# A four-layer graph network on one core: layer 0 takes blocks 1 to 3 ahead of the heavy first block

## The chip, the core and the metric

The kernel runs on one core of a Trainium2 chip. The core has five engines with a queue of instructions each: TensorE (PE in the profile; its weight loads are listed apart as PEld), VectorE (DVE), ScalarE (ACT), GpSimd (POOL) and SyncE (SP, which here only starts transfers). [...] The metric is the device time of one execution in microseconds (us). Before the change it was 1721.15 us, the median of three runs (1717.11 to 1723.85). The profiled execution is longer, 1881.9 us from first to last instruction; times inside the program are read from that one, and the verdict is in the unprofiled times.

## What is computed

There are N = 3327 nodes with 512 features, and a 0/1 adjacency matrix with its entries set very unevenly: the chance of an edge between i and j falls with both indices as (1+i)^-0.5 (1+j)^-0.5, so the first rows have by far the most neighbours. Four layers follow each other, each as x = layernorm(x + layer(x, adj)):

```
layer 0  h = x W (8 heads of 64); e = leaky_relu(f1[i] + f2[j]) where adj[i,j] > 0
         softmax over the neighbours j, out = elu(sum of attention * h[j])
layer 1  relu([x W_self + b, mean of the neighbours W_nb + b] W_comb + b)
layer 2  leaky_relu(mean of the first 64 neighbours W_nb + b) + leaky_relu(x W_line + b)
layer 3  as layer 0, with 4 heads of 128 and quaternion weights
```

The change touches only layer 0 and what comes before it. In layer 0 every row's output is a softmax-weighted sum over that row's neighbours alone, so the blocks of rows can be taken in any order.

## The kernel before

**Tiling.** The 3327 rows are cut into NB = 26 blocks of 128 rows. For every block the kernel builds one or more *edge lists*: the (row, neighbour) pairs of the block, packed into *chunks* of 128 edges. Block 0, with most edges, has three lists of 14 chunks (`HEAVY`, 42 chunks); blocks 1, 2 and 3 have one list of 19, 15 and 13 chunks (47 together), and the later ones fewer, down to 5. The whole has 243 chunks.

**Building the lists** is the generator `structure`. For a block it fetches the adjacency rows in two halves (`fetch`, L839), turns them into 0/1 on ScalarE (`masks`, L846; block 0's go into a tile m0 that is kept, the others into two rotating tiles m), multiplies them with column codes on VectorE (L856), pulls the codes out eight at a time with max and match_replace on VectorE (L874, L876 in segments, L886, L888 over the candidates), and then spreads them over chunks with small matmuls (L902 to L925), ScalarE copies (L905 to L928) and VectorE operations (L932 to L939). Block 0 takes three rounds per segment and 120 slots per row and list, so its lists are long work for VectorE. The generator stops at a `yield` several times per block; the caller decides by `more(n)` how many such steps are placed between other work. By the code, block 0 has 31 steps, blocks 1 to 4 have 7 each, and all others 5.

**The prologue** (the first 220 us of the profile) places, for each block t of 26, one stage of a *projection* (load x, transpose on PE, 8 matmuls L995 in two passes, copies on ScalarE, store to the table t0_d in HBM) and three steps of `structure`. `fused_weights` (layer 1's weights multiplied together, L762) joins at t = 4, and `first_rows` at t = 10. `first_rows` turns m0 into the transposed masks row0 and near0 of block 0, which layers 1 to 3 use: a running count over m0 (L1323), a compare that limits it to the first 64 neighbours (L1326), and 52 transposes (L1332). `finish` then needs all projections and writes the table's two special rows (L1046); only after that may the first gather start.

**Layer 0's loop** goes over *groups* of up to four chunks of one block. A group (`Gat.group`) gathers its chunks' rows from t0_d with indirect transfers issued by GpSimd (L963, one per chunk, into a ring of 22 places `rows`), compares, makes scores with small matmuls (L1165, L1171), takes exponents on ScalarE (L1177, L1178), weighs the gathered rows on VectorE (L1185), and adds them up on PE with two matmuls per chunk in two passes each (L1193). After each group one or two steps of `structure` are placed. When a block's last chunk is in, `layer0_end` follows: normalisation on VectorE and ScalarE with a small piece on GpSimd (L777, L778), a transposition and 8 PE instructions by wn (L762) for layer 1's table t1_d, and for the first ten blocks 8 more by wx. Up to five groups and the ends of earlier blocks are in flight together.

**What sets the order.** Up to the end of layer 0 the program's text does not fix the order within an engine's queue: the framework's scheduler plans it from the dependencies, with the program's order as a preference. One sees it in the trace: the count L1323 is placed at t = 10, but runs at 27.8 us, between the steps of block 0's first list. After layer 0 (`tc.manual_schedule()`) the text's order holds.

**The ring's memory** is lent to the prologue first: m0 lies where places 0 to 3 of the ring are, then the weights, the scores' vectors, layer 1's raw weights, a zero row, and the running count so_far. Some 256 numbers at its end are not lent.

Of the kernel before, what the change touches and what calls it, by code (L numbers as in the profile page):

```python
# [9 lines left out]
BF16 = mybir.dt.bfloat16  # L10
# [8 lines left out]
ALU = mybir.AluOpType  # L19
# [4 lines left out]
P = 128  # L24
# [4 lines left out]
KEEP = 64.0  # L29
# [509 lines left out]
DENSE = 2  # L539
AHEAD = 2  # L540
LATE0 = 16
RING = 22 * 528
MORE = 3072
RANGE = 60.0
# [75 lines left out]
def sparse_path(ctx, tc, flag_i, x, adj, l0_w, l0_a1, l0_a2, l1_w_self, l1_b_self, l1_w_nb, l1_b_nb,  # L620
# [13 lines left out]
    nc = tc.nc  # L634
# [16 lines left out]
    dram = ctx.enter_context(tc.tile_pool(name="s_dram", bufs=1, space=DRAM))  # L651
    keep = pool_in(ctx, "s_keep")

    lists = []
    for b in range(NB):
        parts = HEAVY if b == 0 else ((0, SEGMENTS[b], CAPS[b], SLOTS[b], SEGMENTS[b], 1),)
# [168 lines left out]
    def structure(big, mid, ps, m0):  # L825
# [6 lines left out]
        def fetch(b):  # L832
            ab = abs_[b % len(abs_)]
            for s in range(2):
                w = min(HW, N - s * HW)
                if b == NB - 1:
                    nc.gpsimd.memset(ab[s][96:P, :], 0)
                for p0, p1 in rows_of(b):
                    nc.sync.dma_start(ab[s][p0:p1, :w], adj[b * P + p0:b * P + p1, s * HW:s * HW + w])  # L839
            return ab  # L840

        def masks(b, ab):
            ms = []
            for s in range(2):
                m = m0[:, s * HW:(s + 1) * HW] if b == 0 else big.tile([P, HW], BF16, name="m", bufs=2)
                nc.scalar.activation(m, ab[s], AF.Sign, accum_out=half[:, s, b:b + 1])  # L846
                ms.append(m)
            return ms

        ms = masks(0, fetch(0))  # L850
        yield None
        for b in range(NB):
            ab = fetch(b + 1) if b + 1 < NB else None
            val = big.tile([P, NP], U16, name="val")
            for s in range(2):
                nc.vector.tensor_mul(val[:, s * HW:(s + 1) * HW], ms[s], code[:, s * HW:(s + 1) * HW])  # L856
# [5 lines left out]
            for q, l in enumerate(lists[b]):  # L862
# [7 lines left out]
                for s in range(len(cuts) - 1):  # L870
                    seg = val[:, cuts[s]:cuts[s + 1]]
                    for r in range(rounds):
                        top = cand[:, s * rounds + r, :]
                        nc.vector.max(out=top, in_=seg)  # L874
                        if r + 1 < rounds:
                            nc.vector.match_replace(out=seg, in_to_replace=top, in_values=seg, imm_value=0.0)  # L876
                    if s == (len(cuts) - 1) // 2:
                        if q == 0 and ab is not None:
                            ms = masks(b + 1, ab)
                        yield None  # L880
                cf = cand.rearrange("p s e -> p (s e)")
                sl = mid.tile([P, K + 1], F32, name="sl")
# [34 lines left out]
                for c0 in range(0, L, G):  # L917
# [19 lines left out]
                    with nc.allow_low_precision(reason="whole numbers below 4096"):  # L937
                        nc.vector.tensor_reduce(l.idx[:, c0:c0 + g], eq, AX.X, ALU.add)
                    nc.vector.scalar_tensor_tensor(l.dst[:, c0:c0 + g], l.idx[:, c0:c0 + g], 0.0, v[:, :, 0],  # L939
                                                   ALU.is_gt, ALU.mult)  # L940
            yield b

    def groups(ring, blocks=range(NB)):

# [300 lines left out]
    def lent(n, dtype=F32):  # L1245

        nonlocal free
        at, free = free, free + n * mybir.dt.size(dtype) // 4
        return rows[:, at:free].bitcast(dtype)

    free = 0
# [5 lines left out]
    with ExitStack() as pro:  # L1257
        wp = pool_in(pro, "l0pw", side="right")
        xp = pool_in(pro, "l0px", 2, side="right")
        ps3 = pool_in(pro, "l0pp3", 3, space=PSUM)  # L1260
        ps2 = pool_in(pro, "l0pp2", 2, space=PSUM)
        ps1 = pool_in(pro, "l0pp1", 1, space=PSUM)

        ps = Banks(ps1, po=ps3, tr=ps2)
        banks = Banks(ps1, pv=ps2)
        m0 = lent(NP, BF16)
        made = structure(big, mid, banks, m0)
        w0 = lent(DC * (D + 3 * H0)).rearrange("p (c s o) -> p c s o", c=DC, s=2)
        for c in range(DC):
            for s in range(2):  # L1270
                nc.sync.dma_start(by_heads(w0, c, H0)[:, s],
                                  l0_w[s * H0 // 2:(s + 1) * H0 // 2, c * P:(c + 1) * P, :].rearrange("h p o -> p h o"))
        a0 = lent(2 * D).rearrange("p (s h o) -> p s h o", s=2, h=H0)
        for s, src in enumerate((l0_a1, l0_a2)):
            nc.sync.dma_start(a0[:, s].rearrange("p h o -> p (h o)"), row(src, H0 * OUT0))
        g0 = Gat("g0", t0_d, H0, OUT0, w0, 0)
        next(made)
        score_weights(w0, xp, a0, H0, OUT0)

        def projection(b):  # L1280
            load(xres[b], x, b)
            yield
            xt = transposed(xp, ps, xres[b], g0.xsum, b)
            yield
            pw = g0.products(ps, xt)
            yield
            g0.write(b, xp, pw)

        def fused_weights():

            wc = lent(2 * DC * D).rearrange("p (c o) -> p c o", o=D)
            nc.sync.dma_start(wc, l1_w_comb.rearrange("(c p) o -> p c o", p=P))
            bc = wp.tile([P, D], F32, name="bcomb")
            nc.sync.dma_start(bc, row(l1_b_comb, D))
            bs = wp.tile([P, 2 * DC, 1], F32, name="bs")
            with nc.allow_non_contiguous_dma(reason="two small biases"):
                nc.sync.dma_start(bs[:, :DC, 0], l1_b_self.rearrange("(c p) -> p c", p=P))
                nc.sync.dma_start(bs[:, DC:, 0], l1_b_nb.rearrange("(c p) -> p c", p=P))
            for s, (src, o) in enumerate(((l1_w_self, wx), (l1_w_nb, wn))):
                for i in range(DC):  # L1300
                    raw = xp.tile([P, D], F32, name="raw")
                    nc.sync.dma_start(raw, src[i * P:(i + 1) * P, :])
                    yield
                    rt = transposed(xp, ps, raw)
                    yield
                    po = times(ps, rt, wc[:, s * DC:(s + 1) * DC, :])
                    nc.scalar.copy(o[:, i, :], po)
            pb = ps.tile([P, D], F32, name="po")
            for k in range(2 * DC):
                bb = wp.tile([P, P], F32, name="bb", bufs=2)  # L1310
                nc.vector.tensor_copy(bb, bs[:, k].to_broadcast([P, P]))
                nc.tensor.matmul(pb, bb, wc[:, k, :], start=k == 0, stop=k == 2 * DC - 1)
            nc.vector.tensor_add(bias1, pb, bc)

        def first_rows():

            zero = lent(3 * D, BF16)[0:1, :]
            nc.gpsimd.memset(zero, 0.0)
            for r in range(2):
                nc.sync.dma_start(t1_d[r:r + 1, :], zero)  # L1320
                nc.sync.dma_start(t2_d[r:r + 1, :], zero)
            so_far = lent(NP, I16)
            nc.vector.tensor_tensor_scan(so_far, m0, m0, 0.0, ALU.add, ALU.bypass)  # L1323
            for o in (row0, near0):
                if o is near0:
                    nc.vector.scalar_tensor_tensor(m0, so_far, KEEP, m0, ALU.is_le, ALU.mult)  # L1326
                for c0 in range(0, NB, 8):
                    g = min(8, NB - c0)
                    yield
                    pt = banks.tile([P, 8, P], BF16, name="lp")  # L1330
                    for c in range(g):
                        nc.tensor.transpose(pt[:, c, :], m0[:, (c0 + c) * P:(c0 + c + 1) * P], ident16)  # L1332
                    nc.scalar.activation(o[:, c0:c0 + g, :], pt[:, :g, :], AF.Identity, saturate=False)

        ready, whole = -1, True

        def more(n=1):
            nonlocal ready, whole
            for k in range(n):
                b = next(made, None)  # L1340
                whole = b is not None or ready == NB - 1
                ready = ready if b is None else b

        fused = Stages()
        for t in range(NB):
            work.add(projection(t))
            work.step()
            more(3)
            if t == 4:
                fused.add(fused_weights())  # L1350
            if t == 10:
                fused.add(first_rows())
            fused.step()
        work.drain(more)
        fused.drain(more)
        g0.finish(xp, ps)
        while not whole:
            more()
# [42 lines left out]
                nc.scalar.copy(o[:, :, k * P:(k + 1) * P], pt)  # L1401

    w2lay = ExitStack()
    for k, item in enumerate(groups(pools[0])):
        b = item[0]
        while ready < b:
            more()
        work.add(g0.group(item, pools, accs, layer0))
        work.step()
        more(2 if k % 8 == 0 else 1)  # L1410
        if ready == NB - 1 and wn2 is None:
            listlay.close()
            extra = pool_in(ctx, "s_more").tile([P, MORE], F32, name="gx")
            sp = pool_in(ctx, "s_sel", 3)
            wp = pool_in(w2lay, "l2w")
            wn2 = wp.tile([P, DC, D], F32, name="wn2")
            wl2 = wp.tile([P, DC, D], F32, name="wl2")
            rawp = pool_in(lay, "l2raw", 2)
            work.add(transposed_weights())
# [322 lines left out]
```

## Time and profile before

| What | Value |
|---|---|
| time, median of 3 | 1721.15 us (1717.11 to 1723.85) |
| profiled span | 1881.9 us, mean PE clock 0.929 |
| busy PE / DVE / ACT / POOL | 84% / 66% / 41% / 48% |
| prologue: first gather issued at | 220.8 us |
| layer 0's first summing matmul at | 237.0 us |
| layer 0 to layer 1 (last store of t1_d, a wait of 9.8 us) | 705.8 us |
| gathers in layer 0 | 243, 0.95 us each on POOL |

The busy shares are means over stages of different kinds: in the prologue VectorE is busy nearly without a break, in layers 1 and 2 PE is. A busy PE is not PE at its peak, because matmuls overlap and their ends are modelled: sixteen summing matmuls L1193 in a row take 3.6 us, that is 0.225 us each, though one is listed with 0.41. "PEclk" is the share of the full TensorE clock that was granted in a stretch.

### The profile page before, as it was taken

What the parts mean: (1) busy time and instruction counts of PE and PEld (TensorE: products, weight loads), DVE (VectorE), ACT (ScalarE), POOL (GpSimd) and SP (SyncE); (2) the same over time, 40 slices, a digit from 0 to 9 for tenths busy, and PEclk for the clock granted to TensorE, in tenths of its full rate; (3) what the DMA queues carried; (4) which work ended last, traced back from release to release, by engine and by line L of the source; (5) the groups of instructions that cost most, each with busy time, mean ns of one, the idle gap of its engine ahead of it and who ended that gap; (6) DMA issues with size and microseconds to landing.
All of it is one profiled execution on the core that took longest, in us unless ns stands there. A gap on an engine that the chain in (4) does not pass through costs nothing.

```text
span 1881.9 us, 25357 instructions
## 1 busy us (share of the span) xinstructions
PE 1585.4 (84%) x7947; PEld 1010.9 (54%) x7947; DVE 1245.9 (66%) x3260; ACT 774.0 (41%) x2415; POOL 897.9 (48%) x1007
## 2 busy tenths in 40 slices
PE   5989568999999999998899999598888856877774
PEld 4666456666666664444344444165554545656653
DVE  8999857888978771236577854434433466766786
ACT  4578735566676662211111211022222312444564
POOL 1000266655556524547665433656665233666650
PEclk9999778999999999999999999798999878988888
DMA  8444767777765539879987675878888364666661
GB/s 279 151 133 160 269 211 247 241 229 224 259 194 169 158 118 347 265 232 310 307 262 250 224 280 173 264 231 282 282 292 263 98 195 121 194 191 194 194 187 40
DMA packets 121983, 410.18 MB, mean 218 GB/s; under 512 B 24768, under 2 KB 26304, under 8 KB 121838
## 3 DMA queue, kind: packets, MB, share of 16 engines
q0 software_dynamic: 69584, 286.13, 49.2%
q1 hardware_dynamic: 52254, 122.32, 18.8%
q8 instruction: 65, 1.06, 0.2%
q14 instruction: 80, 0.66, 0.1%
HBM read 360.34 MB, written 48.04 MB: 217 GB/s over the span
## 4 chain that ended last, share of the span: by engine, by line
PE 59%; DVE 20%; issue 9%; ACT 5%; another core or an unknown queue 4%; DMA 3%; POOL 1%; ACTq 0%; SPq 0%; DVEq 0%; POOLq 0%
PE po L762 17%; PE acc L1468 14%; PE acc L1193 14%; PE po L995 7%; DVE gt L1185 4%; DVE cand L874 3%; PE pt L747 2%; PE pg L1165 1%; DVE cand L888 1%; DVE sl L886 1%; DMA gd<-t_d 1%; PE acc L1131 1%; DVE val L856 1%; DMA t_d<-t 1%
## 5 line engine op out<-in xcount | busy, mean ns | idle before, releaser
L963 POOL DMA_INDIRECT gt<-t_d,idx x739 | 730.5, 988 | 748.7 <-DVE cand L888 211.2
L1193 PE MATMUL acc<-gt,sel 128*128 128x264 f32 (+4 forms) x1656 | 435.4, 410 | 34.6 <-issue 29.5
L1193 PEld LDWEIGHTS acc<-gt,sel 128*128 128x128 f32 (+2 forms) x1656 | 319.6, 201 | 118.8 <-issue 65.6
L1185 DVE TENSOR_TENSOR gt<-gt,pg 128x1536 f32<-128x1536 f32 (+3 forms) x129 | 238.8, 1851 | 12.3 <-ACT sel L1180 6.4
L762 PE MATMUL po<-wn,xt 128*128 128x512 f32 x416 | 200.8, 626 | 14.1 <-issue 10.3
L1468 PE MATMUL acc<-gt,sall 128*128 128x512 bf16 x489 | 119.8, 390 | 24.2 <-ACT e L1609 17.5
L995 PE MATMUL po<-w,xt 128*128 128x262 f32 x416 | 106.6, 414 | 34.2 <-issue 28.3
L762 PEld LDWEIGHTS po<-wn,xt 128*128 128x128 f32 x416 | 79.5, 199 | 101.3 <-issue 92.3
L963 POOL DMA_INDIRECT gx<-t_d,idx x107 | 104.4, 976 | 52.8 <-issue 24.3
L874 DVE MAX8 cand<-val 128x8 f32<-128x832 uint16 (+39 forms) x259 | 126.7, 523 | 0.1
L995 PEld LDWEIGHTS po<-w,xt 128*128 128x128 f32 x416 | 84.1, 205 | 56.8 <-issue 33.7
L1468 PE MATMUL acc<-gt,sel 128*128 128x512 bf16 (+3 forms) x486 | 113.3, 379 | 0.0
L995 PE MATMUL po<-gt,xt 128*128 128x268 f32 x416 | 107.8, 404 | 5.6 <-ACT xt L754 4.2
L1468 PEld LDWEIGHTS <-sall 128*128 128x128 fp8e4 x603 | 59.2, 99 | 97.2 <-issue 36.7
L750 ACT COPY xt<-pt 128x512 f32<-128x512 f32 x86 | 50.9, 592 | 132.3 <-PE pt L747 75.3
L1153 ACT ACTIVATE far<-place,nmid 128x384 int16<-128x384 int16 (+3 forms) x138 | 87.4, 636 | 37.6 <-DVE ds L1157 22.9
L1468 PEld LDWEIGHTS <-sel 128*128 128x128 bf16 (+3 forms) x603 | 57.8, 98 | 80.1 <-issue 22.7
L747 PE MATMUL pt<-s_ident,xres 128*128 128x128 f32 x520 | 79.3, 276 | 24.3 <-DMA xres<-in_x_dram 16.0
L1006 ACT COPY tg<-po 128x264 f32<-128x264 f32 (+1 forms) x104 | 39.4, 387 | 141.3 <-PE po L995 62.2
L762 PE MATMUL po<-wx,xt 128*128 128x512 f32 x208 | 94.7, 597 | 2.6 <-ACT vc L928 1.8
L762 PE MATMUL po<-wl,xt 128*128 128x512 f32 x208 | 93.9, 594 | 2.9 <-ACT xt L750 2.1
L1177 ACT ACTIVATE pg<-sc 128x24 f32<-128x24 f32 (+4 forms) x138 | 26.3, 190 | 163.0 <-DVE sc L1176 87.7
(272 smaller groups left out, 2630.4 us busy)
## 6 DMA issues: line engine op xcount, KB each, us to landing
ab<-in_adj_dram SPq DMA_DIRECT2D x25, 832.0 KB
ab<-in_adj_dram SPq DMA_DIRECT2D x25, 831.5 KB
t_d<-t SPq DMA_DIRECT2D x50, 384.0 KB
gt<-t_d POOLq DMA_DIRECT2D x38, 384.0 KB
gt<-t_d,idx POOLq DMA_INDIRECT x739
t_d<-tg SPq DMA_DIRECT2D x25, 264.0 KB
t_d<-tg SPq DMA_DIRECT2D x25, 260.0 KB
gd<-t_d SPq DMA_DIRECT2D x25, 260.0 KB
```

Of the source, the lines that this page charges most:

```text
L747: nc.tensor.transpose(pt[:, c, :], src[:, c * P:(c + 1) * P], ident)
L750: nc.scalar.copy(xt, pt)
L762: nc.tensor.matmul(po, xt[:, c, :], w[:, c], start=c == 0, stop=c == DC - 1)
L874: nc.vector.max(out=top, in_=seg)
L963: nc.gpsimd.indirect_dma_start(out=t[:m, c, :], out_offset=None, in_=table[:, :], in_offset=bass.IndirectOffsetOnAxis(ap=l.idx[:m, c0 + c: ...
L995: nc.tensor.matmul(pw[s], xt[:, c, :], self.w[:, c, s, :], start=c == 0, stop=c == DC - 1)
L1006: nc.scalar.copy(tb[:, s * hh:(s + 1) * hh, :], by_head[:, :, 1:])
L1153: nc.scalar.activation(far[:, :g * P], place[:, c0 * P:(c0 + g) * P], AF.Abs, bias=l.nmid, scale=2.0)
L1177: nc.scalar.activation(w[:, :g], sc[:, :g, 0], AF.Exp)
L1185: nc.vector.tensor_mul(Gc[:, :, :OUT], Gc[:, :, :OUT], w[:, :g].rearrange("p c (h o) -> p (c h) o", o=1).to_broadcast([P, g * H, OUT]))
L1193: nc.tensor.matmul(accs[b][s], S[:m, c, :], G[:m, c, s * hh * M:(s + 1) * hh * M], start=at + c == 0, stop=at + c == chunks_of[b] - 1)
L1468: nc.tensor.matmul(accs[b], S[:m, c, :], G[:m, c, k * D:(k + 1) * D], start=at + c + k == 0, stop=k == 2 and at + c == n - 1)
```

## The change

Layer 0 takes its blocks in the order 1, 2, 3, 0, 4, 5, ... and the lists are built in the same order. So block 0's three long lists are built after those of three blocks of middling size, and three blocks come to their ends before block 0's 42 chunks are summed. Because block 0's mask m0 is then still needed when the others are under way, and ring places are filled in another order, two things are added: the limited mask goes to a place of its own (over so_far) in place of overwriting m0, and two memsets on GpSimd fill memory of the ring which otherwise would be read, though not used, before anything had been written there.

```diff
+FIRST = 3
+    order = [*range(1, FIRST + 1), 0, *range(FIRST + 1, NB)]
...
-        ms = masks(0, fetch(0))
+        ms = masks(order[0], fetch(order[0]))
         yield None
-        for b in range(NB):
-            ab = fetch(b + 1) if b + 1 < NB else None
+        for k, b in enumerate(order):
+            ab = fetch(order[k + 1]) if k + 1 < NB else None
...
-                            ms = masks(b + 1, ab)
+                            ms = masks(order[k + 1], ab)
...
-            yield b
+            yield k
...
-            zero = lent(3 * D, BF16)[0:1, :]
-            nc.gpsimd.memset(zero, 0.0)
+            zeros16 = lent(3 * D, BF16)
+            nc.gpsimd.memset(zeros16, 0.0)
+            zero = zeros16[0:1, :]
...
             so_far = lent(NP, I16)
+            nc.gpsimd.memset(rows[:, free:], 0.0)
+            near = so_far.bitcast(BF16)
             nc.vector.tensor_tensor_scan(so_far, m0, m0, 0.0, ALU.add, ALU.bypass)
             for o in (row0, near0):
                 if o is near0:
-                    nc.vector.scalar_tensor_tensor(m0, so_far, KEEP, m0, ALU.is_le, ALU.mult)
+                    nc.vector.scalar_tensor_tensor(near, so_far, KEEP, m0, ALU.is_le, ALU.mult)
...
-                        nc.tensor.transpose(pt[:, c, :], m0[:, (c0 + c) * P:(c0 + c + 1) * P], ident16)
+                        src = m0 if o is row0 else near
+                        nc.tensor.transpose(pt[:, c, :], src[:, (c0 + c) * P:(c0 + c + 1) * P], ident16)
...
-    for k, item in enumerate(groups(pools[0])):
-        b = item[0]
-        while ready < b:
+    for k, item in enumerate(groups(pools[0], order)):
+        while ready < order.index(item[0]):
             more()
```

## The prediction

> **What bounds the kernel now.** The change touches only the prologue (0 to 220 us of the profile) and layer 0 (220 to 705 us), so I read those stages, not the whole. First the engines' busy time by stretches of 50 us; the columns are the stretch, its length, then PE, PEld, DVE, ACT and POOL busy (with counts), the granted PE clock, the DMA share and GB/s.
>
> ```profile
> 50.00:100.00 50.00, 47.18 (x233) 33.23 (x233) 47.66 (x198) 25.70 (x101) 0.00 (x0) 0.96 0.40 129
> 100.00:150.00 50.00, 42.69 (x282) 30.50 (x281) 47.97 (x169) 38.63 (x128) 0.00 (x0) 0.97 0.44 146
> 150.00:200.00 50.00, 48.90 (x326) 35.47 (x326) 49.70 (x186) 44.20 (x148) 0.00 (x0) 1.00 0.58 188
> 200.00:250.00 50.00, 23.26 (x181) 17.14 (x180) 33.75 (x113) 27.36 (x72) 21.47 (x22) 0.71 0.79 266
> ```
>
> Between 50 and 200 us VectorE is busy 145 of 150 us: the prologue is its list-building. In the timeline it has five gaps worth a mention from 17 to 226 us, 3.2 us together and 1.12 the longest. PE looks as full, but that is modelled; its real need is smaller (416 L995 at 0.225 us = 94 us, 64 L762 at 0.43 us = 28 us). Then the waits of the prologue, and GpSimd's first one (waiter, releaser: total, times, longest):
>
> ```profile
> PE p L902 <- DVE dg L900: 13.7, 4, 5.6
> SPq L839 <- ACT m L846: 23.4, 5, 7.9
> POOL gt L963 <- DVE cand L888: 211.2, 1, 211.2
> ```
>
> PE waits for VectorE where a list's row counts go into matmuls (L902). GpSimd does nothing for 211 us. Its named releaser had long been done; what really opened it is the store of the table's special rows, issued at 215.6 us. Last, layer 0's start, in finer stretches, same columns:
>
> ```profile
> 237.00:252.00 15.00, 7.38 (x32) 5.67 (x31) 3.19 (x3) 2.44 (x5) 8.97 (x9) 0.73 0.76 246
> 252.00:267.00 15.00, 9.90 (x77) 8.04 (x76) 8.45 (x22) 5.03 (x13) 10.07 (x11) 0.84 0.68 220
> 267.00:311.00 44.00, 38.64 (x268) 31.06 (x265) 33.55 (x76) 19.91 (x57) 27.32 (x29) 0.90 0.71 213
> 311.00:330.00 19.00, 16.24 (x105) 12.48 (x104) 16.42 (x44) 10.16 (x33) 11.36 (x12) 0.82 0.82 256
> 360.00:400.00 40.00, 35.47 (x223) 25.02 (x223) 31.96 (x78) 22.92 (x60) 24.26 (x28) 0.96 0.75 245
> 450.00:500.00 50.00, 47.79 (x271) 33.02 (x270) 45.19 (x110) 35.27 (x97) 27.97 (x32) 0.97 0.75 245
> ```
>
> While block 0's 42 chunks go through (237 to about 314 us) no engine is full and the PE clock is below 1; from 400 us on PE and VectorE both are near full. That slack, with no block's end to fill it, is what the new order can use.
>
> [...] the gathers' rows of 0.95 us say nothing of the landing, the first group being used 11 us after its issue.
>
> **Part 1, the order of the lists.** Steps of the first four blocks: 31+7+7+7 = 52, whichever comes first; the prologue places 78 and a few more, so from block 4 on the program text is the same. VectorE's work moves inside the prologue: block 0's multiplications ran at 17.0 and 20.4 us and the next block's at 97.9 and 99.2, so its lists take some 80 us; the next ones began at 119.8 and 134.4 us, so 15 to 20 us each. The sum is unchanged. As VectorE has hardly a gap before, permuting its work gains next to nothing by itself: 0 us. It could lose, if an adjacency block comes late: blocks 1 to 3 use one each 15 us, where block 0 gave its follower 80. A block is 1.66 MB; at the 350 to 370 GB/s that 10 to 30 us show it is 5 us of transfer, and the tile is free once its mask (two times 1.6 us on ACT) is done, early in the block ahead. So about 15 us are there for 5 + 3 us: hidden, up to 8 us if the load queues behind the 2 MB of W_comb issued at 18.5 us. I take 0, ends -8 and +8 (the first if PE, stalled less by the long lists' L902 early on, ends its projections sooner; PE was the chain from 165 to 207 us).
>
> **Part 2, m0, near and the memsets.** The count (7.08 us) and the compare (3.62 us) keep their shapes: 0. The mask of block 0 comes some 30 us later, the count with it; its transposes ran only from 120 us on, so this is hidden. Writing near beside m0 takes away the compare's wait on the first 26 transposes; VectorE shows no gap there, so it is worth 0. The two memsets have no row of their size. Nearest are a GpSimd memset of 512 numbers (0.52 us) and an iota of 3328 (2.89 us), so 1536 bf16 and 256 numbers are 0.5 to 2 us together, and GpSimd is idle until 220 us: 0. Behind them wait the zero rows' stores, needed in layer 1.
>
> **Part 3, the order in layer 0.** Prices: PE per chunk 4 x 0.225 (L1193) + 12/4 x 0.044 (twelve L1165 in 0.53 us) + 0.10 (four L1171 in 0.39) = 1.13 us. GpSimd per chunk 0.95 + 0.30 = 1.25 us. VectorE per group 1.85 (L1185) + 0.33 + 0.24 + 0.18 = 2.6 us. A block's end: PE 0.6 + 3.5 + 3.5 = 7.6 us; VectorE five sweeps of 0.69 and small ones = 4.3 us. Before, groups 1 to 12 are block 0: PE needs 42 x 1.13 = 47 us, GpSimd 52, elapsed 77. Groups 13 to 25 are blocks 1 to 3 with the ends of 0, 1 and half of 2: PE 53 + 19 = 72 us, elapsed 86 (to about 400). After, groups 1 to 13 are blocks 1 to 3 with the ends of 1 and 2: 53 + 15 = 68 us; groups 14 to 25 are block 0 with the end of 3: 47 + 8 = 55 us. Total PE need is 119 us before and 123 after (half an end more), for 163 us elapsed: two ends, 15 us of PE, move from a full stretch into a slack one. All of it saved would be 15 us. But [...] VectorE does not have that slack: over 267 to 330 us it was busy 50 of 63 us, and two ends bring 8.6 more: 58.6 of 63. The first group's landing (220 to 237 us) and the PE gaps of 243 to 252 us come before any end and stay. ScalarE takes about 6 us more per end, of 30 busy in those 63; that has room. I take a third, 5 us gained, ends +3 (VectorE binds, ends and list steps contend for the single PSUM tiles they share, and ACT, stuck on a mask as at 282 to 289 us, holds the ends too) and -15. The group count falls from 76 to 75 since the ring wraps elsewhere: 2.6 us of VectorE less 2 for longer groups, under 1 us.
>
> **Part 4, the rest.** The last blocks and all of layers 1 to 3 keep their text; layer 1's first items need every block's t1_d, so they begin after the last store either way. 0. Sum: 0 + 0 - 5 = -5 us of 1721: 1716.
>
> **The rivals.** (a) *No more than that, inside 0.5% (8.6 us)*: my forecast, 1716 us. For it: unchanged sums on a VectorE that is hardly ever free. (b) *Clearly faster*: all the slack is filled [...] (252 to 330 us lost 2.4 + 4.4 + 3.4 = 10 us to the clock, half of it reachable): -15 - 5, less a little because PE can't be full: -18, about 1703 us. For it: PE idle there; against: VectorE's 50 of 63. (c) *Slower*: the scheduler plans all of prologue and layer 0 anew from estimates, the lists' short latencies at the start open gaps on VectorE (8 us), and the ends push list-building and gathers back (+3, and some 4 more for GpSimd waiting on an end's L777 between gathers): +15, 1736 us. For it: such placements cost PE 13.7 us at L902; against: the early transfers have time.
>
> **How the numbers follow.** Chances: (a) 0.42, (b) 0.36, (c) 0.22. The range goes from 1700, just past (b), to 1736, (c)'s value; outside I leave about 0.1 on each side. Faster by over 0.5% 0.36, within 0.42, slower 0.22.
>
> **What would show it.** Right: the first gather still near 220 us (between 212 and 228); summing matmuls of layer 0 with L762 among them before 300 us; PEclk of 267 to 330 us above 0.9; group 25's last sum at about 393 us; layer 1's wait for t1_d 5 us sooner, and from there an unchanged distance to the end. Wrong: gaps on VectorE before 60 us that end in a mask or an adjacency load; a first gather that moves by over 8 us; or a layer 0 whose first 25 groups take as long as before, with VectorE full.

## The result, and the profile after

The changed kernel takes 1706.6 us (median of 4 runs, 1705.80 to 1707.92) against 1721.51 us before (4 runs, 1717.11 to 1723.85): ratio 0.9917, 95% interval [0.9896, 0.9938], so 15 us faster. The forecast was 1716 us within 0.5%; the outcome is past that bound and lies nearer to rival (b), 1703 us.

One thing has to be known before the traces are compared. The profile that the prediction reads came from a run of 1883.9 us; the times on record are near 1722 us. In the runs below the same kernel takes about 1722 us on some chips and 1875 us or more on others, so that profile is taken to be from one of the slower kind. (Each chip was used for one set of runs, so its lasting property cannot be told from a state it was in for a time.) A trace of the kernel before was therefore taken on a 1722 us chip (span 1721.1 us), and that one is compared with the changed kernel's (span 1704.1 us). In the changed kernel's listing the lines touched by both stand 3 higher (L777 is L780, L821 is L824, L963 is L966, L1193 is L1196), and layer 1's first transfer L1454 is L1460.

The changed kernel in the stretches that were shown of before (columns: stretch, length, PE, PEld, DVE, ACT, POOL busy with counts, PE clock, DMA share, GB/s):

```profile
50.00:100.00 50.00, 45.01 (x229) 31.16 (x228) 49.14 (x221) 28.12 (x114) 0.00 (x0) 0.99 0.60 207
100.00:150.00 50.00, 44.38 (x231) 31.96 (x230) 48.27 (x191) 27.80 (x107) 0.00 (x0) 1.00 0.23 78
150.00:200.00 50.00, 46.05 (x297) 32.42 (x296) 47.10 (x168) 40.51 (x133) 0.00 (x0) 0.93 0.48 151
...
267.00:311.00 44.00, 41.83 (x295) 31.88 (x296) 41.24 (x95) 26.08 (x76) 34.19 (x37) 0.93 0.82 250
311.00:330.00 19.00, 19.00 (x123) 13.28 (x122) 17.31 (x39) 14.69 (x38) 14.31 (x16) 1.00 0.87 278
267.00:330.00 63.00, 60.83 (x417) 45.16 (x418) 58.55 (x133) 40.77 (x113) 48.50 (x52) 0.95 0.83 258
```

The kernel before on the 1722 us chip, the last three of the same stretches:

```profile
267.00:311.00 44.00, 38.42 (x312) 31.20 (x310) 40.55 (x102) 25.85 (x76) 33.34 (x36) 1.00 0.90 290
311.00:330.00 19.00, 13.18 (x58) 8.91 (x57) 10.05 (x22) 7.86 (x17) 11.93 (x14) 0.60 0.77 235
267.00:330.00 63.00, 51.60 (x365) 40.11 (x363) 50.60 (x124) 33.71 (x92) 45.27 (x49) 0.88 0.86 273
```

The prologue is as full of VectorE as it was (144.5 of 150 us). The greater part of the difference lies in 311 to 330 us: before, PE, VectorE and ScalarE drop together and the PE clock falls to 0.60; after, there is no hole. The waits named in the prediction, after (waiter, releaser: total, times, longest):

```profile
POOL gt L966 <- DVE some L893: 210.6, 1, 210.6
PE p L905 <- DVE dg L903: 5.3, 3, 2.2
SPq L842 <- ACT m L849: 22.5, 7, 7.2
```

GpSimd still does nothing for 211 us and then starts. Three marks place the gain (us from the start). The first pair is the kernel before and the changed one on one chip, one trace each; the last column is the trace of the changed kernel on record.

| Mark | before | after | after, on record |
|---|---|---|---|
| first gather | 220.9 | 222.0 | 220.5 |
| layer 1's first transfer (L1454, L1460) | 658.9 | 644.8 | 642.6 |
| end of the program | 1721.1 | 1707.8 | 1704.1 |

The prologue gives nothing: the first gather is 1.1 us later, and in three traces of the changed kernel it lies anywhere from 220.5 to 223.7 us. Layer 0 gives all: it is 15.2 us shorter from its first gather on, so layer 1 starts 14.1 us sooner. From layer 1's start to the end it is 1062.2 us before and 1063.0 after.

What makes the hole of 311 to 330 us is seen in the timelines of the kernel before, 1722 us chip, at the end of block 0 (start, duration, engine, line, operation; in brackets the idle time before it and who ended it). VectorE first:

```profile
307.31 0.18 DVE L769 BATCH_NORM_AGGREGATE mv<-st 128x2 f32<-128x6 f32 x1
...
310.30 0.18 DVE L914 TENSOR_TENSOR dl<-p,dl 128x25 bf16<-128x25 f32 x1 [0.24 <-ACT dl L913]
318.82 0.16 DVE L821 SCALAR_TENSOR_TENSOR nm<-mv,rs 128x1 f32<-128x1 f32 x1 [8.34 <-POOL rs L778]
```

GpSimd in the same time, where rs is made from mv:

```profile
314.53 0.95 POOL L963 DMA_INDIRECT gt<-t_d,idx  x1 [0.30 <-PE acc L1193]
315.78 0.94 POOL L963 DMA_INDIRECT gt<-t_d,idx  x1 [0.30 <-issue]
316.80 0.18 POOL L777 TENSOR_SCALAR rs<-mv 128x1 f32<-128x1 f32 x1
317.25 0.91 POOL L963 DMA_INDIRECT gt<-t_d,idx  x1 [0.27 <-issue]
318.19 0.59 POOL L778 TENSOR_TENSOR rs<-rs,s_mhalf 128x1 f32<-128x1 f32 x1
```

And TensorE behind both:

```profile
320.82 1.12 PE L747 MATMUL pt<-s_ident,xres 128*128 128x128 f32 x4 [5.45 <-ACT xres L822]
```

VectorE has the variance, mv, at 307.5 us. The little computation on GpSimd that follows (rs, 0.18 + 0.59 us) stands in GpSimd's queue behind eight gathers, 1.25 us apart, and comes out at 318.8 us. VectorE had been given only 3 us of other work between mv and nm; it stands still for 8.34 us, and ScalarE and TensorE behind it. In the changed kernel the first end is block 1's:

```profile
279.24 0.17 DVE L772 BATCH_NORM_AGGREGATE mv<-st 128x2 f32<-128x6 f32 x1
...
287.93 0.14 DVE L903 CAST dg<-dgs 128x1 bf16<-128x1 f32 x1
288.15 0.16 DVE L824 SCALAR_TENSOR_TENSOR nm<-mv,rs 128x1 f32<-128x1 f32 x1
```

GpSimd there:

```profile
287.27 0.18 POOL L780 TENSOR_SCALAR rs<-mv 128x1 f32<-128x1 f32 x1
287.54 0.58 POOL L781 TENSOR_TENSOR rs<-rs,s_mhalf 128x1 f32<-128x1 f32 x1
```

So rs comes at 288.1 us, almost 9 us after mv. The delay on GpSimd has not gone; but 9 us of other VectorE work lies between, so VectorE does not wait for it.

### The profile page after: what moved, and what is told of

It is laid out like the page before. It is cut to its first block, busy times and chain, and to the rows that moved or that the text cites. A ratio compares the mean times of both kernels' runs of the same rounds, so it can differ in the third digit from the quotient of the medians.

```text
span 1704.1 us, 25362 instructions
## 1 busy us (share of the span) xinstructions
PE 1523.7 (89%) x7947; PEld 981.5 (58%) x7947; DVE 1243.4 (73%) x3256; ACT 773.2 (45%) x2411; POOL 911.9 (54%) x1008
## 4 chain that ended last, share of the span: by engine, by line
PE 61%; DVE 16%; DMA 11%; ACT 6%; issue 3%; POOL 2%; SPq 0%; DVEq 0%; ACTq 0%; POOLq 0%
PE po L765 20%; PE acc L1196 15%; PE acc L1474 14%; DMA gt<-t_d,idx 7%; PE po L998 6%; PE pt L750 2%; DVE cand L877 2%; DVE gt L1188 2%; DMA gx<-t_d,idx 2%; POOL gt L966 2%; PE pg L1168 2%; DMA gd<-t_d 1%; DVE cand L891 1%; DVE sl L889 1%; ACT h L1213 1%
## 5 line engine op out<-in xcount | busy, mean ns | idle before, releaser
L966 POOL DMA_INDIRECT gt<-t_d,idx x739 | 742.1, 1004 | 578.9 <-DVE some L893 210.6
L1196 PE MATMUL acc<-gt,sel 128*128 128x264 f32 (+4 forms) x1656 | 413.7, 399 | 27.1 <-issue 20.1
L1196 PEld LDWEIGHTS acc<-gt,sel 128*128 128x128 f32 (+2 forms) x1656 | 311.4, 195 | 97.8 <-issue 42.9
L1188 DVE TENSOR_TENSOR gt<-gt,pg 128x1536 f32<-128x1536 f32 (+2 forms) x128 | 238.6, 1864 | 6.3 <-ACT gt L1181 2.9
L765 PE MATMUL po<-wn,xt 128*128 128x512 f32 x416 | 192.9, 607 | 3.8 <-ACT xt L753 3.8
L765 PEld LDWEIGHTS po<-wn,xt 128*128 128x128 f32 x416 | 77.2, 193 | 89.4 <-issue 78.4
L966 POOL DMA_INDIRECT gx<-t_d,idx x107 | 107.6, 1006 | 38.6 <-issue 14.9
L877 DVE MAX8 cand<-val 128x8 f32<-128x832 uint16 (+38 forms) x259 | 125.7, 522 | 0.0
L1474 PEld LDWEIGHTS <-sel 128*128 128x128 bf16 (+3 forms) x603 | 57.9, 98 | 80.0 <-issue 22.7
L998 PE MATMUL po<-w,xt 128*128 128x262 f32 x416 | 96.2, 384 | 1.6 <-ACT xt L757 1.6
L765 PE MATMUL po<-wl,xt 128*128 128x512 f32 x208 | 94.0, 594 | 2.9 <-ACT xt L753 2.9
L765 PE MATMUL po<-wx,xt 128*128 128x512 f32 x208 | 94.3, 596 | 1.3 <-ACT xt L753 1.2
L750 PEld LDWEIGHTS pt<-s_ident,xres 128*128 128x128 f32 x520 | 63.8, 143 | 46.2 <-issue 31.2
L849 ACT ACTIVATE m<-ab 128x1664 bf16<-128x1664 int32 x50 | 80.4, 1607 | 20.5 <-DMA ab<-in_adj_dram 15.6
```

The lines of the kernel that those rows point to most:

```text
L750: nc.tensor.transpose(pt[:, c, :], src[:, c * P:(c + 1) * P], ident)
L765: nc.tensor.matmul(po, xt[:, c, :], w[:, c], start=c == 0, stop=c == DC - 1)
L966: nc.gpsimd.indirect_dma_start(out=t[:m, c, :], out_offset=None, in_=table[:, :], in_offset=bass.IndirectOffsetOnAxis(ap=l.idx[:m, c0 + c: ...
L998: nc.tensor.matmul(pw[s], xt[:, c, :], self.w[:, c, s, :], start=c == 0, stop=c == DC - 1)
L1188: nc.vector.tensor_mul(Gc[:, :, :OUT], Gc[:, :, :OUT], w[:, :g].rearrange("p c (h o) -> p (c h) o", o=1).to_broadcast([P, g * H, OUT]))
L1196: nc.tensor.matmul(accs[b][s], S[:m, c, :], G[:m, c, s * hh * M:(s + 1) * hh * M], start=at + c == 0, stop=at + c == chunks_of[b] - 1)
```

## The experiments

**The kernel before again, on a 1875 us chip.** No edit; a measure of how far two runs of one kernel differ, and a trace.

> The kernel before, once more, for a second profile of it. Every theory expects 1721 us within 0.3%. Theory (slack filled by early ends): a profile whose span is near the unprofiled time still shows PE in 252 to 330 us at less than 90% of full speed, no L762 among the summing matmuls before some 330 us, and the step from layer 0 to layer 1 about 12 to 15 us later than the changed kernel has it. Rival (the gain lies in layers 1 to 3, by the state in which the memory and the PE clock are left): the step comes at the same time in both and the difference grows later.

Measured: 1872.78 us, ratio 0.9997 [0.9975, 1.0018]. The 1721 us that were expected did not come: this chip is of the slower kind. Layer 1's first transfer stands at 692.5 us, where the 1722 us chip had 658.9.

**The two small edits alone, order as before.** The changed kernel, which keeps near beside m0 and the two memsets, with

```diff
-FIRST = 3
+FIRST = 0
```

> The changed kernel with FIRST = 0: old order of lists and of layer 0, only the two memsets and the separate place of near are left. Theory: ratio 1.000 to the kernel before (0.997 to 1.003). Rival (the compare that no longer writes over m0, or any new planning of the schedule, makes the gain): 0.991 to 0.995.

Measured on the 1875 us chip: 1884.5 us, ratio 1.0054 [1.0032, 1.0075]. This is outside the expected 0.997 to 1.003. The first gather came at 224.9 us against 220.6, layer 1's first transfer at 697.0 against 692.5: in these two traces the whole loss up to layer 1 lies in the prologue, and layer 0 is as long as before. So this plan is not quite free there, though the instructions are: the next experiment contains them too and shows nothing. Why the prologue ends later, no run here tests. It does show that edits meant to be free can move the time by half a per cent.

**Lists in the new order, the loop in the old one.** The changed kernel with

```diff
-    for k, item in enumerate(groups(pools[0], order)):
+    for k, item in enumerate(groups(pools[0])):
```

> Lists built in the order 1, 2, 3, 0, but layer 0 takes the blocks as before, 0 first. Theory (only the order of layer 0 counts): 1.000 (0.997 to 1.003), first gather within 3 us of 220. Rival (the order of the lists makes the gain, by a smoother prologue): 0.992, with a first gather that is no earlier than in the changed kernel.

Measured on the 1875 us chip: ratio 0.9993 [0.9970, 1.0017]. The lists' order is worth nothing alone.

**The loop in the new order, lists in the old one.** The kernel before with near, the memsets and

```diff
-    for k, item in enumerate(groups(pools[0])):
-        b = item[0]
-        while ready < b:
+    for k, item in enumerate(groups(pools[0], order)):
+        while ready < max(item[0], 3):
```

> Lists built as before, block 0 first, but layer 0 takes the blocks in the order 1, 2, 3, 0. Theory: the whole gain, 0.992 (0.989 to 0.995). Rival (lists): 1.000.

Measured on the 1875 us chip: 1891.67 us, ratio 1.0084 [1.0051, 1.0117], slower. My expectation fell. The loss up to layer 1 is nearly all in layer 0 (its end at 707.1 us against 692.5, the first gather at 222.1 against 220.6). Either the parts need each other, or the chip matters.

**The pair as it is, on a 1722 us chip**, with a trace of each.

> The changed kernel once more, beside the kernel before on one chip. The last call's chip took 1875 us for the kernel before, where the times on record say 1721, and there the new order of layer 0 alone cost 0.8% and the lists' order alone nothing. If the gain is the change's own: ratio 0.992 (0.989 to 0.995) whatever level the chip has. Rival (the gain belongs to the quicker level[...] and the slower level gives it back): 0.992 where the kernel before takes 1721, 1.000 to 1.010 where it takes 1875.

> The kernel before, with a profile, on the same chip as the changed one. Every theory expects the level of its own timed runs. If that is the quicker level, the theory of filled slack expects the first 25 groups of layer 0 to end some 10 to 15 us later than in the changed kernel, with PE at under 90% busy from 237 to 330 us.

Measured: 1708.05 us changed, beside 1724.08 us for the kernel before (11 runs): ratio 0.9911 [0.9888, 0.9934]. The trace of the kernel before is of a single further run, 1722.97 us. The gain repeats. The first 25 groups of layer 0 end at 376.7 us before and 369.8 changed, 7 us sooner and not 10 to 15; PE is busy 84% of 237 to 330 us before, as expected. These two traces showed the wait on rs, and the next four kernels, all run on one more 1722 us chip, test it.

**The changed kernel, its parts, and the wait alone.** The fourth kernel leaves the order of blocks and of lists as it was; it only puts two more places (each a `yield` of the end's generator, at which other work is planned in) between the issue of rs on GpSimd and its use on VectorE, at block 0's end:

```diff
-    def rstd(fin, mv):
+    def rstd(fin, mv, more=0):
...
         nc.gpsimd.tensor_tensor(rs, rs, mhalf, ALU.pow)
-        yield
+        for _ in range(1 + more):
+            yield
...
-        e, mv, rs = yield from g0.summed(fin, acc, x1)
+        e, mv, rs = yield from g0.summed(fin, acc, x1, 2 if b == 0 else 0)
```

> The changed kernel beside its parts on one chip. If the gain comes from the wait of VectorE on GpSimd's rs at the end of block 0 (8.3 us in the kernel before), and holds on every chip: ratio 0.990 to 0.994, layer 1's first gather 13 to 15 us sooner than in the kernel before. Rival, the gain depends on the chip: on a chip where the kernel before takes about 1875 us the ratio is 0.997 to 1.008, as the loop's order alone gave there (1.0084).

> Lists in the order 1, 2, 3, 0, the loop of layer 0 in the old order 0, 1, 2, 3. Both theories: the prologue's work is only permuted and block 0 still ends first, so the wait on rs stays: ratio 0.998 to 1.002. Below 0.995 the lists' order itself would be a cause of the gain.

> Lists in the old order, the loop of layer 0 in the order 1, 2, 3, 0. If the loop's order alone makes the gain, through the wait on rs: 0.990 to 0.995 and no wait over 4 us on rs at the first block's end. Rival (the two parts need each other, or the chip decides): 1.000 to 1.010, as on the first chip, where it was 1.0084.

> The kernel before, with two more places between the issue of rs on GpSimd and its use on VectorE, at block 0's end alone. If that wait (8.3 us of VectorE, 7.9 of ScalarE, 5.4 of TensorE, and a TensorE clock of 0.60 in 311 to 330 us) is what the change removes: the wait on rs below 1 us, PEclk of 311 to 330 us at 0.9 or more, ratio 0.992 to 0.996. Rival, ends that fill slack make the gain, and the wait costs nothing by itself: ratio 0.999 to 1.001.

Measured, beside 1721.55 us for the kernel before (PE busy is of the 390 us from 250 to 640 us):

| Kernel | median us | ratio, 95% | layer 1's start | PE busy |
|---|---|---|---|---|
| before (its trace is of the other 1722 us chip) | 1721.55 | | 658.9 | 369.8 |
| changed | 1707.49 | 0.9919 [0.9906, 0.9933] | 642.5 | 378.7 |
| lists only | 1721.62 | 0.9999 [0.9988, 1.0010] | 658.3 | 366.2 |
| loop only | 1713.89 | 0.9954 [0.9941, 0.9968] | 650.6 | 376.1 |
| later use of rs only | 1714.86 | 0.9958 [0.9944, 0.9973] | 654.4 | 372.2 |

The stretch of 311 to 330 us of the kernel with lists only, its TensorE there, and VectorE's waits on rs from 220 to 640 us (total, times, longest):

```profile
311.00:330.00 19.00, 9.32 (x55) 6.70 (x52) 9.08 (x21) 7.18 (x16) 12.64 (x16) 0.73 0.74 217
```

```profile
322.88 1.12 PE L750 MATMUL pt<-s_ident,xres 128*128 128x128 f32 x4 [9.30 <-ACT xres L825]
```

```profile
DVE nm L824 <- POOL rs L781: 22.4, 10, 10.5
```

The same stretch of the kernel with the later use, the end of its block 0, and its waits on rs, with those of the kernel before (1722 us chip) below:

```profile
311.00:330.00 19.00, 18.46 (x138) 14.72 (x137) 17.59 (x36) 11.20 (x29) 14.79 (x17) 0.91 0.88 280
```

```profile
308.86 0.18 DVE L769 BATCH_NORM_AGGREGATE mv<-st 128x2 f32<-128x6 f32 x1
...
322.30 0.59 POOL L778 TENSOR_TENSOR rs<-rs,s_mhalf 128x1 f32<-128x1 f32 x1
...
327.65 0.15 DVE L822 SCALAR_TENSOR_TENSOR nm<-mv,rs 128x1 f32<-128x1 f32 x1
```

```profile
DVE nm L822 <- POOL rs L778: 16.4, 11, 3.0
```

```profile
DVE nm L821 <- POOL rs L778: 20.2, 10, 8.3
```

Block 0's nm comes at 327.65 us there with no wait in front of it, and a change of two places in the plan, no instruction more or less, gains 0.42% [0.27, 0.56]. That is 4.6 to 9.6 us, 6.7 in the medians; in the traces layer 1 starts 4.5 us sooner than in the kernel before, 3.9 sooner than with lists only. Its rival (ratio 0.999 to 1.001) is out, and the hole closes just where the wait was, as expected beforehand. So that wait is a cause by itself, and by the medians about half of the change's gain, 6.7 of 14.1 us. One reservation stays: other work is planned anew as well, and the two small edits, with theirs, cost 0.54% on the slower chip. Short waits on rs at later ends also stay, 16.4 us in all.

The loop's order alone gives about as much (7.7 us, just outside the expected 0.990 to 0.995). There, too, the long wait is gone (3.3 us is the longest), so this may be the same gain in another way; no run parts them. The lists' order gives nothing alone, but beside the loop's order 6.4 us more (1713.89 to 1707.49). In the loop-only trace TensorE still has holes that the changed kernel's has not:

```profile
253.74 0.45 PE L1168 MATMUL pg<-g0own,ds 128*128 128x16 bf16 x9 [5.67 <-DVE gt L1188]
296.56 1.05 PE L750 MATMUL pt<-s_ident,xres 128*128 128x128 f32 x4 [1.90 <-ACT nmid L911]
396.89 0.43 PE L1168 MATMUL pg<-g0own,ds 128*128 128x16 bf16 x9 [2.35 <-DVE gt L1188]
```

These three are 9.9 us; the changed kernel on that chip has one hole over 0.8 us between 240 and 560 us, of 3.94. The first of them follows a wait of VectorE for a gather (4.13 us). From 220 to 240 us it is the changed kernel that waits longer (16.2 us against 13.4), so the holes do not add up to the 6.4 us.

One estimate places the gains. PE's busy time times the granted clock, summed over the four stretches from 237 to 330 us (cut at 252, 267 and 311), is 70.2 us before, 68.5 with lists only, 77.0 with the loop only, 78.1 with the later use and 81.1 changed. So most of each gain is TensorE work that gets done in these 93 us.

**Is the rest block ends in the slack?** Lists in the new order, loop in the old, and the later use of rs: if the loop's order only removes the wait, this has the whole gain.

> Lists in the order 1, 2, 3, 0, the loop of layer 0 in the old order, and two more places before the use of rs at block 0's end (the wait removed without the loop's order). If the loop's order matters only because it removes that wait, this has the gain of the whole change: ratio 0.990 to 0.994 beside the kernel before. Rival, ends of blocks between the chunks of block 0 give the rest: 0.994 to 0.998, as the later use alone gave (0.9958), since the lists' order alone gave nothing (0.9999). On a chip of the 1875 us kind these marks don't hold, and only the sign is read.

**A version that might beat both**: the changed kernel with one more place at every block's end (the same edit, `g0.summed(fin, acc, x1, 1)`).

> The changed kernel with one more place before the use of rs at every block's end; there VectorE waits 15 to 16 us in all on rs, eleven times, 3.3 us the longest, and ScalarE 5 us behind it. If these waits cost time as the long one did: ratio 0.986 to 0.990 beside the kernel before. Rival, TensorE is full there (49 to 50 of every 50 us from 300 to 550 us) and the waits are off the path: 0.990 to 0.994, the same as the changed kernel.

Both ran on another chip of the slow kind, beside 1891.52 us for the kernel before: ratios 1.0040 [1.0015, 1.0066] and 1.0043 [1.0019, 1.0066]. Neither gains there, so neither question is answered for a 1722 us chip. In both traces VectorE stands 15 to 16 us early in layer 0, up to 248 us (the profile calls the releaser "remote"), and the first summing matmul comes at 254 us, where the kernel before has it at 237 on the 1875 us chip. No trace of the kernel before was taken on this chip, so it stays open whether the edits or the chip make that.

How much there is to gain on a slow chip can be read from the traces of the kernel before. The use of rs in the kernel before on the 1875 us chip, from 220 to 640 us:

```profile
L821 DVE SCALAR_TENSOR_TENSOR nm<-mv,rs x18: 138/150/161, 335.7 to 635.3; 128x1 f32<-128x1 f32 x18
```

```profile
  POOL rs L778: 4.4, 5
```

Five waits, 4.4 us in all, and one of 2.2 us at block 0's end that the profile puts to no engine: the long one is not there. The profile that the prediction read has the same place with a wait of 3 us:

```profile
330.56 0.18 DVE L769 BATCH_NORM_AGGREGATE mv<-st 128x2 f32<-128x6 f32 x1
...
336.08 0.59 POOL L778 TENSOR_TENSOR rs<-rs,s_mhalf 128x1 f32<-128x1 f32 x1
336.71 0.16 DVE L821 SCALAR_TENSOR_TENSOR nm<-mv,rs 128x1 f32<-128x1 f32 x1 [2.98 <-POOL rs L778]
```

So rs stands in the queue there too, but behind three gathers instead of eight: it comes 5.9 us after mv, against 11.3 on the 1722 us chip. GpSimd from 240 to 300 us, first on the 1875 us chip, then on the 1722 us chip, the same kernel (POOL busy with its count, PE clock, DMA share, GB/s):

```profile
240.00:300.00 60.00, 36.42 (x39) 0.80 0.73 228
```

```profile
240.00:300.00 60.00, 45.51 (x48) 0.97 0.88 290
```

On the first chip GpSimd issues 39 gathers in these 60 us (1.54 us each) and has idle gaps of up to 3.5 us between them, most of all until summing matmuls free places of the ring; on the second 48, which is one per 1.25 us, the pace of issue itself (0.95 us each and 0.30 us idle before the next). That a GpSimd with idle gaps has fewer gathers standing before rs fits these numbers, but no run tests it. Layer 0 ends 34 us later on the first chip.

## Why the prediction was right, and where not

The 1706.6 us lie within the range of 1700 to 1736 us. The forecast inside it, no more than 0.5%, did not come; that the range, which reached past rival (b), still held the result is in part luck, since about half of the gain came by a wait that no part of the working has.

**Bound.** That layer 0's first 100 us have slack, and that the change can use it, held. But it was not the slack that I priced: from 237 to 267 us PE idled 12.7 us in the profile read and 3.7 us on the 1722 us chip, where the hole lies in 311 to 330. Marks that held: the first gather at 220.5 us; L765 among the summing matmuls before 300 us (8 of them from 250 to 300); an unchanged distance from layer 1's start to the end; a PE clock of 0.95 in 267 to 330 us. Group 25's last sum was forecast near 393 us; the 356 summing matmuls of the first four blocks are through at 367.7 us after (369.8 in the second trace) and 376.7 before on the 1722 us chip, 7 to 9 us sooner instead of 5. The mark of 393 itself was read from the slower chip.

**Part 1, lists' order: 0.** Right. Alone it is 0.9999. PE's wait for row counts did shrink as the lower end had it, from 11.9 us before (1722 us chip) to 5.3, while another wait on the lists grew (L914 on sl, 9.7 us; L911, the same line before, 3.0). VectorE has no gap between 11 and 60 us in the changed kernel. ScalarE waits for adjacency blocks 15.6 us in all, five times, but 11.7 of them are for the very first block, as in the kernel before (11.4); the longest of the others is 2.5. The late transfer I feared did not come.

**Part 2, near and memsets: 0.** Their durations are hidden as said: the memsets take 1.37 and 0.30 us before 10 us. (The first has a row in the profile before, L1318 with 1536 numbers and 1.37 us, which I overlooked.) But 1.0054 in the one run that had them alone, with a first gather 4.3 us later, says that a zero for instructions isn't a zero for the plan.

**Part 3, the order in layer 0: -5. The term that was mis-sized**: it measured -14.1 us at layer 1's start (658.9 to 644.8). Two steps of its working failed.
- "VectorE does not have that slack": the sum of 58.6 of 63 us came true, 58.55 were measured in 267 to 330 us, from 50.60 before. But that did not hold back two thirds of the gain. Its 58.6 us of work still fitted into the 63; PE was busy 60.8 of the 63. That a busy sum came near the length of the stretch was no reason to take a third.
- The wait on rs, by the medians about half of the gain, is in no step. The working of rival (c) had the pair of instructions, L777 between gathers, but took the cost to be the gathers' delay; it was L777 that stood behind them. In the profile that I read it could be seen, but small: 2.98 us at block 0's end, 7.3 us in all. Its size of 8.3 us could not. What could be seen as well is that the profiled span, 1881.9 us, was 9% over the times. That should have widened the chance of things which only a faster run shows.

**Part 4, the rest: 0.** Right: 1062.2 and 1063.0 us.

**Rivals.** (b) said 15 us of filled slack and 5 of clock. The amount is nearly right. Both of its terms are there, smaller: over 267 to 330 us PE's busy time rose by 9.2 us (51.60 to 60.83); at full clock that is, as an estimate from the lines above, 46.3 to 57.9 us, so 2.4 us more by the clock. The 5 was my estimate: in the profile that I read the PE clock was 0.50 from 220 to 237 us, with PE busy 3.4 of the 17, and 0.73 to 0.90 in the stretches from 237 to 311; what sets it, no run here shows. But some half of the gain was no slack in search of work; it was one wait. (c)'s +15 did not come on the 1722 us chips. The changed kernel as it stands was not timed on a slow chip, so whether it gains there stays open; the loop's order alone loses 0.8% there, and on the other slow chip the version with places added loses 0.4%.

**Open.** What the lists' order adds to the loop's (6.4 us), beyond the holes shown, and how much of the other half is block ends in slack: the runs meant to part them fell on a chip of the slow kind, where they do not answer it.

## What to carry to other kernels

A small operation on GpSimd in the middle of a VectorE chain waited here behind every gather placed ahead of it in the queue. Look at the time from its input to its output (11 us here for 0.8 us of work), not at its duration, and put that much other VectorE work between; here two places in the plan gave nearly half of what a new order of all work gave. And before costing a stage from a profile, compare the profiled span with the times: where they differ by 9%, the waits on record may not be those of the runs that are timed.

## What the runs showed that I had not expected

- One kernel takes about 1722 us on two chips, 1875 and 1892 us on two others. Between the traces of 1870.8 and 1721.1 us the prologue is alike (first gather at 220.6 and 220.9 us), layer 0 is 34 us longer, with 39 gathers issued in 60 us against 48, and layers 1 to 3 are 116 us longer. The mean PE clock is 0.927 against 0.962. What the cause is can't be read here: in the slower traces the landings of the gathers carry no time.
- The ranking of versions turns with the chip: the loop's order alone is 1.0084 on one and 0.9954 on the other.
- Over the 19 us in which VectorE waits 8.3 us for 0.8 us of work on GpSimd, the PE clock is 0.60; it is 0.91 with the wait moved. It does not follow the wait's length: with lists only the wait is 10.5 us and the clock 0.73.
